# Near-row search end in a written-out order, bias by chunks, near sums from product 20, and a carry row outside the rank pool

## The chip, the cores and the metric

The kernel runs on one core of a Trainium2 chip. The metric is the device time of one execution in microseconds (us). Three timed executions of the kernel before took 1072.16, 1079.40 and 1079.82 us; their median, 1079.4 us, is the time before. A separate execution was profiled; all times of single instructions come from it.

## The reference

Four graph layers in a row on N = 2708 nodes with 128 features, each followed by a residual sum and a layer norm. The adjacency matrix `adj` is dense in memory, and every layer multiplies by it. Layer 0 is the one around this change:

```python
def _lap_mul(A, x):
    d = 1.0 / jnp.sqrt(jnp.sum(A, axis=-1))
    return d[:, None] * (A @ (d[:, None] * x))
z = jax.nn.leaky_relu(_lap_mul(A, x) @ W1 + b1, negative_slope=0.1)
sq = jnp.sum(z * z, axis=-1)
d2 = jnp.maximum(sq[:, None] + sq[None, :] - 2.0 * (z @ z.T), 0.0)
S = jnp.exp(-jnp.sqrt(d2 + 1e-10) / 2.0)
S = jnp.where(ranks_of_minus_S < 4, S, 0.0)      # the 4 nearest rows of each row
out = _lap_mul(S + A, x) @ W2 + b2
x = layernorm(x + out)
```

Layer 1 is an attention layer, `H = A @ (att @ (x W))` with `att = den / (A @ den)` and `den = exp(leaky_relu(r_i + c_j))`. Layer 2 is a normalized product with `A`, a linear map and a bias; layer 3 is `relu([x, A @ x] @ W.T + b)`.

## The kernel before, in words

**Tiling.** Rows lie in T = 22 tiles of 128 (the last, tile 21, has 20 rows). The columns of `adj` are cut into C = 6 chunks of 512, 512, 512, 512, 384 and 276; a chunk holds 4, 4, 4, 4, 3 and 3 tiles. Six row tiles of `adj` stay in SBUF (`res`); the other sixteen stream through a ring of four slots (`ring`), one slot a panel of four row tiles by one chunk.

**Search (lines 672 to 708).** For each row tile TensorE makes a row block of keys (L689, L699), ScalarE copies it out (L700, three `key` buffers), and VectorE takes the eight largest (L701, `near`) and where they lie (L702, `where`). The last row tiles searched are 16, 17, 18, 19 and 20. `weigh(ts)` turns the four best keys of a group of tiles into similarities `sim` (L596 and L597 on VectorE, L598 to L600 on ScalarE), adds them to the degree (L602, L603), takes the inverse root `d2inv` (L604, L605), scales the rows, `y2` (L607 on GpSimd, or L260 on VectorE for the last group), and stores them to the DRAM tensor `y2_rows` (L615, L619: GpSimd's queue, or ScalarE's for the last group). `others(ts)` (L561 to L589) takes the row itself out of the four and writes the three others' indices back to `where`. `weigh` is called for tiles 0 to 16, 17 to 19, and 20 to 21. Here a scheduler places VectorE's instructions in an order of its own.

**Second product of layer 0 (`by_panels`, lines 202 to 229 and 956 to 1013).** For each chunk, 22 products with `y2` are accumulated; a list of due times, `Due`, counts one tick for each product, and work is hung on ticks (`at(n, f)`). The order of TensorE, VectorE and ScalarE is as written here. `sum_near(t)` gathers the three other near rows of each row of tile t from `y2_rows` by indirect DMA on GpSimd (L729) and sums them on VectorE (L738, L742). It is due at tick `24 + 23 t // 5`. When a chunk's products are done, `end_pass2` sets the tick `n` of its `finish`, never before the tick of its last tile's near sum plus 3; `finish` adds the near sums into the chunk's accumulator on TensorE (`add_near`, L749). At later ticks follow the linear map and the norm (`norm0`: L780, L785), the transposes (L798), the column terms (`find_c`, L852, L857) and the comparisons by which layer 1 ranks its columns (L884, L894, L902, L907). `add_bias(b2_sb)` (L774, L265) adds the bias to all rows of `xs` in one VectorE instruction ahead of this loop.

**Rank stage (lines 1077 to 1475).** It sorts rows into blocks and sums carry rows over the lines of `adj` in two halves (`add_line`, L1360). `end_half(h)` copies the sums from PSUM into `heads` (L1380, L1381), a tile of the pool `rank` with both halves side by side, and `send_half` (L1389) moves them by four DMAs into `carry`: half 0 on ScalarE's queue, half 1 on SP's at the end of the stage.

**Block loop (`block_layer`).** 44 steps: TensorE makes `num` (L1627), ScalarE its inverse (L1481, L1484), VectorE three operations on it (L1491, L1495, L1498), TensorE adds up (L1506). Its tiles come from the pool `own`, which takes the space of `rank` once that is closed, so a first write there waits for the last readers of what lay there. Then `two_layers` runs layers 2 and 3 with `by_panels`. The tile `m_rows` has the tag `hT`, one buffer that `hT`, `head`, `first` and `hot_in` use one after the other.

Of the kernel before, what the change touches and what calls it, by code (L numbers as in the profile page):

```python
# [26 lines left out]
DIST_EPS = 1e-10  # L27
# [3 lines left out]
class Due:  # L31
# [5 lines left out]
    def at(self, n, f, *args):  # L37
        self.work.append((n, len(self.work), f, args))
        self.work.sort(key=lambda w: w[:2])
# [13 lines left out]
def kernel(  # L53
# [16 lines left out]
    nc = tc.nc  # L70
    N, D = x.shape
    assert D == P
    T = (N + P - 1) // P
# [13 lines left out]
    HALF = N // 2  # L87
# [13 lines left out]
    chunk_tiles = [range(a // P, (a + w + P - 1) // P) for a, w in zip(starts, cw)]  # L101
# [24 lines left out]
    xs = big.tile([P, T, D], F32, tag="xs", name="xs")  # L126
# [23 lines left out]
    def row_tile(name):  # L150
        return big.tile([P, T * D], F32, tag="hT", name=name)
# [112 lines left out]
    def add_bias(b):  # L264
        nc.vector.tensor_add(xs, xs, b[:, None, :].to_broadcast([P, T, D]))  # L265
# [95 lines left out]
    sim = near_pool.tile([P, T, TOPK], F32, tag="sim", name="sim")  # L361
    y2_rows = dram.tile([N, D], F32, tag="y2_rows", name="y2_rows")
    xw_rows = dram.tile([N, D], F32, tag="xw_rows", name="xw_rows")
    with tc.tile_pool(name="knn", bufs=1) as knn:
        nsq = knn.tile([P, T], F32, tag="nsq", name="nsq")
# [195 lines left out]
        def others(ts, engine):  # L561

            t0, t1 = ts[0], ts[-1] + 1
            n = t1 - t0
            wf, eq, sm = near[:, t0:t1, :TOPK], near[:, t0:t1, TOPK:], sim[:, t0:t1, :]
            own = own_sim[:, t0:t1]
            four = slot_e[:, : 4 * n].rearrange("p (t k) -> p t k", k=4)
            three = slot_e[:, : 3 * n].rearrange("p (t k) -> p t k", k=3)  # L570
            nc.scalar.copy(wf, where[:, t0:t1, :TOPK])
            nc.vector.tensor_tensor(
                eq, wf, node[:, t0:t1, None].to_broadcast([P, n, TOPK]), op=ALU.is_equal
            )
            engine.tensor_mul(four, eq, sm)  # L575
            engine.tensor_add(own, four[:, :, 0], four[:, :, 1])
            for k in (2, 3):
                engine.tensor_add(own, own, four[:, :, k])
            for k in (1, 2, 3):
                engine.tensor_add(eq[:, :, k], eq[:, :, k - 1], eq[:, :, k])  # L580
            for v in (wf, sm):
                engine.tensor_sub(three, v[:, :, 1:], v[:, :, :3])
                engine.tensor_mul(three, three, eq[:, :, :3])
                engine.tensor_add(v[:, :, :3], v[:, :, :3], three)
            engine.tensor_copy(where[:, t0:t1, TOPK : TOPK + 3], wf[:, :, :3])
            for t in ts:
                engine.tensor_scalar(
                    lone[: pw[t], t : t + 1], eq[: pw[t], t - t0, 3:], -1.0, 1.0, op0=ALU.mult, op1=ALU.add
                )  # L589

        def weigh(ts):

            t0, t1 = ts[0], ts[-1] + 1
            nr, sm = near[:, t0:t1, :TOPK], sim[:, t0:t1, :]

            nc.vector.tensor_add(nr, nr, nsq[:, t0:t1, None].to_broadcast([P, t1 - t0, TOPK]))  # L596
            nc.vector.tensor_scalar(nr, nr, 0.0, DIST_EPS, op0=ALU.min, op1=ALU.subtract)  # L597
            nc.scalar.activation(sm, nr, AF.Ln, scale=-1.0)  # L598
            nc.scalar.activation(sm, sm, AF.Exp, scale=0.5)
            nc.scalar.activation(sm, sm, AF.Exp, scale=-0.5)  # L600
            dd = d2inv[:, t0:t1]
            nc.vector.tensor_reduce(dd, sm, AX.X, ALU.add)  # L602
            nc.vector.tensor_add(dd, dd, deg[:, t0:t1])  # L603
            nc.scalar.activation(dd, dd, AF.Ln)  # L604
            nc.scalar.activation(dd, dd, AF.Exp, scale=-0.5)  # L605
            if t1 < T:
                nc.gpsimd.tensor_mul(  # L607
                    y2[:, t0:t1, :], xs[:, t0:t1, :], d2inv[:, t0:t1, None].to_broadcast([P, t1 - t0, D])
                )
            else:  # L610
                scale_rows(y2, xs, d2inv, ts)
                spread(y2[:, FULL, :])
            full = min(t1, FULL)
            queue = nc.gpsimd if t1 < T else nc.scalar
            queue.dma_start(  # L615
                y2_rows[t0 * P : full * P, :].rearrange("(t p) d -> p t d", p=P), y2[:, t0:full, :]
            )
            if full < t1:
                queue.dma_start(y2_rows[FULL * P :, :], y2[:LAST, FULL, :])  # L619
            else:  # L620
                for a in range(t0, t1, 11):
                    others(range(a, min(a + 11, t1)), nc.gpsimd)

        QUARTER = N // 4
        assert N % 4 == 0 and CW < QUARTER <= 2 * CW
# [45 lines left out]

        ready = [load_panel(g, 0) for g in range(G)]
        tc.keep_in_program_order(nc.scalar.preload_act_table_set("natural_log_exp_and_others"))
        with tc.tile_pool(name="keys", bufs=3) as keys:

            for n, t in enumerate([*range(4, S), *range(4), *range(S, FULL)]):
                p = pw[t]
                if n == 1:
                    best = search_few()
                if n == 3:  # L680
                    join_few(best)
                z2 = small.tile([P, P], F32, tag="z", name="z2")
                nc.scalar.mul(z2[:, :p], zT[:, t * P : t * P + p], 2.0)

                key = keys.tile([P, N], F32, tag="key", name="key")
                pks = [acc_tile() for _ in range(C)]
                def norms(c):
                    cs = cols[c]
                    nc.tensor.matmul(pks[c][:p, : cw[c]], lhsT=ones3[:, :p], rhs=nsq3[:, cs], start=True, stop=False)  # L689


                if n:
                    for c in range(C):
                        norms(c)
                for c in range(C) if n else (5, 3, 2, 4, 1, 0):
                    if not n:
                        norms(c)
                    cs = cols[c]
                    nc.tensor.matmul(pks[c][:p, : cw[c]], lhsT=z2[:, :p], rhs=zT[:, cs], start=False, stop=True)  # L699
                    nc.scalar.copy(key[:p, cs], pks[c][:p, : cw[c]])  # L700
                nc.vector.max(near[:p, t, :], key[:p])  # L701
                nc.vector.max_index(where[:p, t, :], near[:p, t, :], key[:p])  # L702
                if t == T - 6:
                    weigh(range(0, T - 5))
                if t == T - 3:
                    weigh(range(T - 5, T - 2))
            weigh(range(T - 2, T))
            others(range(T - 2, T), nc.vector)

    psum.close()  # L710
    acc_pool = psum.enter_context(tc.tile_pool(name="acc1", bufs=3, space=bass.MemoryType.PSUM))
# [59 lines left out]
    spare = near.rearrange("p t k -> p (t k)")  # L771
    few_n, rk_f, neg_r = (spare[:, n * T : (n + 1) * T] for n in range(3))
    nc.vector.memset(rows_d, 0.0)
    add_bias(b2_sb)  # L774
    rk = rk_pool.tile([P, T], F32, tag="rk", name="rk")

    def norm0(ts, raw=False):
# [177 lines left out]

    due = Due()
    at = due.at
    near_at = [24 + (23 * t) // 5 for t in range(T)]
    for t in range(T):
        at(near_at[t], sum_near, t)  # L960
    at(20, nc.vector.memset, rk_f, float(OOB))

    ended = [-16]
# [98 lines left out]
    rows = {}  # L1062
# [14 lines left out]
    with tc.tile_pool(name="rank", bufs=1) as rank:  # L1077
        def rtile(shape, name, dt=F32):
            return rank.tile([P] + shape, dt, tag=name, name=name)
# [295 lines left out]
        def end_half(h):  # L1375

            if not carries:
                carries.append(big.tile([P, NQ * P], F32, tag="y", name="carry"))
            tot = heads[:, h * span : (h + 1) * span]
            nc.scalar.copy(tot[:, : edges[4] - edges[3]], banks[h][:, : edges[4] - edges[3]])  # L1380
            nc.scalar.copy(tot[:64, edges[4] - edges[3] :], banks[h][:64, edges[4] - edges[3] : span])  # L1381
            if h == 0:
                send_half(h, tot, nc.scalar)

        def send_half(h, tot, queue):

            for g in range(4):
                w = edges[g + 1] - edges[g]
                queue.dma_start(  # L1389
                    carries[0][HEADS : HEADS + 2 * NCH, h * HALF + edges[g] : h * HALF + edges[g + 1]],  # L1390
                    tot[32 * g : 32 * g + 2 * NCH, :w],
                )
# [39 lines left out]

        work["groups"] = 0
        nc.vector.tensor_reduce(lone_part, lone, AX.X, ALU.add)
        heads = rtile([2 * span], "heads")
        loaded, held = [0], [0]

        def line(n):
# [24 lines left out]
        ]  # L1463
        for f, *args in turns:
            f(*args)
        end_half(1)
        carry = carries[0]
        assert loaded[0] == 2 * S and held[0] == 2 * (FULL - S) and work["groups"] == 6
        xws, lw = work["xws"], work["lw"]
        load(0)  # L1470
        load(1)
        send_half(1, heads[:, span:], nc.sync)
        for c in range(C):
            nc.sync.dma_start(res[few(c), FULL - S, cols[c]], adjT[FULL * P :, cols[c]])
        order.close()
# [35 lines left out]
    WIDE = 2 * CW  # L1511
    NARROW = HALF - WIDE
    assert 0 < NARROW <= CW

    m_rows = row_tile("m_rows").rearrange("p (t d) -> p t d", d=D)
    mT = m_rows.rearrange("p t d -> p (t d)")[:, :N]

    mixed = carry.rearrange("p (t d) -> p t d", d=D)
    EARLY = HALF // P
# [301 lines left out]
```

## Time and profile before

| | us |
|---|---|
| median of three executions | 1079.4 (1072.16 to 1079.82) |
| profiled execution, its own time | 1053.01 |
| its span, first to last instruction | 1051.3 |
| PE busy | 981.7 (93%) |
| DVE busy | 637.8 (61%) |
| ACT busy | 331.6 (32%) |
| POOL busy | 265.4 (25%) |

PE is TensorE, PEld its weight load, DVE VectorE, ACT ScalarE, POOL GpSimd, SP the engine whose queue issues most DMAs. A busy share is an average over stages. In the profiled execution the search ends at about 294 us, the second product of layer 0 runs from 288 to 424, the rank stage to 493, the block loop to about 715, and the rest is layers 2 and 3. A line of the timeline gives the start in us, the duration, the engine, the line of the kernel, the operation, output and inputs with their sizes, and in brackets the idle time before it with the work that ended the wait.

### The profile page before, as it was taken

The page shows a single profiled execution, that of the slowest core. Times are in us where ns is not written, and L with a number is a line of the kernel's source. Part 1 is how long each engine was busy: PE and PEld are TensorE (multiplying, and loading weights), DVE is VectorE, ACT ScalarE, POOL GpSimd, SP SyncE. Part 2 cuts the span into 40 slices and gives each one's busy share as a digit, 9 for nine tenths or more (in the row PEclk, how much of TensorE's full clock was granted, in tenths as well). Part 3 has the DMA queues.
Part 4 walks back from the last instruction along what each step waited for, and adds up shares of the span by engine and source line. Part 5 has one row for each costly group of instructions (what it writes and reads, how often), then busy time and mean ns, then how long its engine had stood idle before and what let it go on. Part 6 is the DMA issues. An engine that isn't in the chain of part 4 may idle for free.

```text
span 1051.3 us, 11657 instructions
## 1 busy us (share of the span) xinstructions
PE 981.7 (93%) x3773; PEld 481.5 (46%) x3773; DVE 637.8 (61%) x1358; ACT 331.6 (32%) x609; POOL 265.4 (25%) x339
## 2 busy tenths in 40 slices
PE   0898999999997998799899999999999999999996
PEld 0346554444443566554333333334445544564444
DVE  5885438999954668764999999994121121222222
ACT  0000125555501245503777777662010100010000
POOL 4000000000377774007666444420121100000000
PEclk9899999999999999699899999999999999999998
DMA  9997350000086756596565455566665956584652
GB/s 337 355 364 262 113 174 1 0 1 1 1 269 198 227 182 208 201 410 206 144 168 154 138 138 169 137 172 221 201 206 161 316 164 220 146 277 163 220 173 70
DMA packets 102001, 191.00 MB, mean 182 GB/s; under 512 B 14022, under 2 KB 43342, under 8 KB 101930
## 3 DMA queue, kind: packets, MB, share of 16 engines
q1 hardware_dynamic: 83896, 152.34, 43.5%
q0 software_dynamic: 17728, 37.62, 12.9%
q8 instruction: 32, 0.52, 0.2%
q14 instruction: 39, 0.32, 0.1%
q10 hardware_dynamic: 306, 0.20, 0.1%
HBM read 214.80 MB, written 4.16 MB: 208 GB/s over the span
## 4 chain that ended last, share of the span: by engine, by line
PE 72%; DVE 16%; DMA 6%; ACT 2%; issue 2%; POOL 1%; SPq 1%; POOLq 0%; DVEq 0%; ACTq 0%
PE acc L204 34%; PE hacc L1506 10%; PE num L1627 10%; PE acc L428 7%; DVE where L702 6%; DVE near L701 5%; DMA res<-in_adjT 3%; PE acc L1360 3%; DMA got<-y_rows,where 1%; PE mis L285 1%; PE acc L699 1%; DMA part<-in_adjT 1%; DVE both L483 1%; POOL ring L125 1%; PE mis L1090 1%
## 5 line engine op out<-in xcount | busy, mean ns | idle before, releaser
L1068 POOL DMA_INDIRECT ring<-in_adjT,slot_i x88 | 93.7, 1065 | 96.2 <-PE num L1627 77.4
L1627 PE MATMUL num<-ring,lw 128*64 128x512 f32 (+1 forms) x528 | 112.7, 560 | 5.3 <-DVE err L1491 4.7
L1506 PE MATMUL hacc<-inv,xws 128*128 128x512 f32 (+1 forms) x264 | 112.0, 560 | 0.3 <-DVE inv L1498 0.3
L699 PE MATMUL acc<-zT,z 128*128 128x512 f32 (+2 forms) x252 | 102.2, 552 | 0.0
L1481 ACT ACTIVATE inv<-num,plain 128x1024 f32<-128x1024 f32 x88 | 80.6, 916 | 59.8 <-PE num L1627 42.9
L253 POOL TENSOR_TENSOR rstd<-rstd,minus_half 128x4 f32<-128x4 f32 (+1 forms) x18 | 17.3, 961 | 311.8 <-DVE rstd L252 311.8
L234 ACT COPY gb<-acc 128x512 f32<-128x512 f32 (+2 forms) x18 | 9.6, 536 | 249.4 <-PE acc L204 249.4
L700 ACT COPY key<-acc 128x512 f32<-128x512 f32 (+2 forms) x126 | 67.1, 535 | 55.1 <-issue 27.9
L1506 PEld LDWEIGHTS hacc<-inv,xws 128*128 128x128 f32 x264 | 46.7, 190 | 78.1 <-issue 33.7
L204 PE MATMUL acc<-ring,y 128*128 128x512 f32 (+2 forms) x192 | 81.3, 554 | 0.5 <-issue 0.5
L1491 DVE TENSOR_TENSOR err<-inv,num 128x1024 f32<-128x1024 f32 x88 | 74.7, 854 | 11.0 <-ACT inv L1484 9.8
L729 POOL DMA_INDIRECT got<-y_rows,where x66 | 71.7, 1087 | 26.3 <-issue 9.1
L1498 DVE SCALAR_TENSOR_TENSOR inv<-gb,g_inv,inv 128x1024 f32<-128x1024 f32 x88 | 77.0, 913 | 0.1
L204 PE MATMUL acc<-ring,xs 128*128 128x512 f32 (+2 forms) x192 | 76.7, 542 | 0.0
L204 PE MATMUL acc<-ring,carry 128*128 128x512 f32 (+2 forms) x192 | 74.5, 542 | 0.0
L204 PE MATMUL acc<-ring,m_rows 128*128 128x512 f32 (+2 forms) x192 | 74.3, 542 | 0.0
L1495 DVE SCALAR_TENSOR_TENSOR inv<-err,inv 128x1024 f32<-128x1024 f32 x88 | 72.5, 862 | 0.1
L699 PEld LDWEIGHTS acc<-zT,z 128*128 128x128 f32 x252 | 45.8, 190 | 50.4 <-issue 45.0
L1484 ACT ACTIVATE inv<-inv 128x1024 f32<-128x1024 f32 x88 | 67.6, 768 | 2.8
L575 POOL TENSOR_TENSOR slot_e<-near,sim 128x44 f32<-128x44 f32 (+2 forms) x3 | 0.7, 243 | 267.8 <-DVE d2inv L603 265.7
L1627 PEld LDWEIGHTS num<-ring,lw 128*64 128x64 f32 x528 | 36.8, 138 | 62.5 <-issue 44.4
L701 DVE MAX8 near<-key 128x8 f32<-128x2708 f32 x21 | 62.3, 2965 | 2.7 <-ACT key L700 2.7
(376 smaller groups left out, 1369.8 us busy)
## 6 DMA issues: line engine op xcount, KB each, us to landing
ring<-in_adjT SPq DMA_DIRECT2D x74, 1024.0 KB
ring<-in_adjT SPq DMA_DIRECT2D x20, 677.0 KB
ring<-in_adjT SPq DMA_DIRECT2D x17, 768.0 KB
part<-in_adjT SPq DMA_DIRECT2D x12, 1024.0 KB
ring<-in_adjT SPq DMA_DIRECT2D x17, 552.0 KB
more<-in_adjT SPq DMA_DIRECT2D x10, 677.0 KB
res<-in_adjT SPq DMA_DIRECT2D x4, 1280.0 KB
part<-in_adjT SPq DMA_DIRECT2D x3, 768.0 KB
```

Source lines behind the costliest of these rows:

```text
L204: nc.tensor.matmul(accs[c][: lhsT.shape[-1], :w], lhsT=lhsT, rhs=src, start=start, stop=stop)
L428: nc.tensor.matmul(accs[c][:, : cw[c]], lhsT=y[:, i, :], rhs=src[:, : cw[c]], start=first, stop=last)
L699: nc.tensor.matmul(pks[c][:p, : cw[c]], lhsT=z2[:, :p], rhs=zT[:, cs], start=False, stop=True)
L701: nc.vector.max(near[:p, t, :], key[:p])
L729: nc.gpsimd.indirect_dma_start(out=got[:p, :], out_offset=None, in_=y2_rows[:, :], in_offset=bass.IndirectOffsetOnAxis(ap=where[:p, t, k : ...
L1068: nc.gpsimd.indirect_dma_start(out=rows[i][:KC, n, :], out_offset=None, in_=adj_half[:, :], in_offset=bass.IndirectOffsetOnAxis(ap=slot_i[ ...
L1481: nc.scalar.activation(inv, num[:, :w], AF.Ln, scale=plain[:, 0:1], bias=plain[:, 1:2])
L1491: nc.vector.tensor_mul(err, inv, num[:, :w])
L1495: nc.vector.scalar_tensor_tensor(inv, err, 2.0, inv, op0=ALU.subtract, op1=ALU.mult)
L1498: nc.vector.scalar_tensor_tensor(inv, gb[:, col : col + w], g_inv[:, q : q + 1], inv, op0=ALU.max, op1=ALU.mult)
L1506: nc.tensor.matmul(haccs[:, o:e], lhsT=xws[:, q, :], rhs=inv[:, o:e], start=(q == 0), stop=(q == NQ - 1))
L1627: nc.tensor.matmul(num[n * (BJ + 2) : (n + 1) * (BJ + 2), o:e], lhsT=lw[:, 2 * q + n, :], rhs=rows[i][:, n, c0 + o : c0 + e], start=True, ...
```

## The change

Five things are edited.

1. `weigh` is cut into `weigh_near` (L596 to L600; it now writes to `sim` and leaves `near` as it was), `find_d2` and `keep_y2`. From row tile 16 on, VectorE's order is the written one (`manual_schedule` for the vector engine alone). `weigh_near` of a group stands between the L701 and the L702 of the group's last searched tile; for tiles 20 and 21, `find_d2` and `keep_y2` stand there too. `others` of tiles 0 to 16 follows `keep_y2` of its group, and that of tiles 17 to 19 is called after `weigh_near` of the last group.
2. The bias is added by chunks, `add_b2`, six VectorE instructions hung on the tick of the chunk's first near sum.
3. Near sums are due from tick 20 on instead of 24, 4.8 ticks apart instead of 4.6.
4. `heads` becomes a list: half 0 in a tile of half the former size in the pool `rank`, half 1 in a part of `m_rows`.
5. `m_rows` and `mT` are therefore made before `end_half(1)`.

```diff
-        def weigh(ts):
+        def weigh_near(ts):
             t0, t1 = ts[0], ts[-1] + 1
             nr, sm = near[:, t0:t1, :TOPK], sim[:, t0:t1, :]
-            nc.vector.tensor_add(nr, nr, nsq[:, t0:t1, None].to_broadcast([P, t1 - t0, TOPK]))
-            nc.vector.tensor_scalar(nr, nr, 0.0, DIST_EPS, op0=ALU.min, op1=ALU.subtract)
-            nc.scalar.activation(sm, nr, AF.Ln, scale=-1.0)
+            nc.vector.tensor_add(sm, nr, nsq[:, t0:t1, None].to_broadcast([P, t1 - t0, TOPK]))
+            nc.vector.tensor_scalar(sm, sm, 0.0, DIST_EPS, op0=ALU.min, op1=ALU.subtract)
+            nc.scalar.activation(sm, sm, AF.Ln, scale=-1.0)
             nc.scalar.activation(sm, sm, AF.Exp, scale=0.5)
             nc.scalar.activation(sm, sm, AF.Exp, scale=-0.5)
+
+        def find_d2(ts):
+            t0, t1 = ts[0], ts[-1] + 1
             dd = d2inv[:, t0:t1]
-            nc.vector.tensor_reduce(dd, sm, AX.X, ALU.add)
+            nc.vector.tensor_reduce(dd, sim[:, t0:t1, :], AX.X, ALU.add)
...
+        def keep_y2(ts):
+            t0, t1 = ts[0], ts[-1] + 1
             if t1 < T:
...
                 queue.dma_start(y2_rows[FULL * P :, :], y2[:LAST, FULL, :])
-            else:
-                for a in range(t0, t1, 11):
-                    others(range(a, min(a + 11, t1)), nc.gpsimd)
...
+        ends = ExitStack()
...
+                if t == T - 6:
+                    ends.enter_context(tc.manual_schedule(engines={nc.vector.engine}))
                 nc.vector.max(near[:p, t, :], key[:p])
+                if t == T - 6:
+                    weigh_near(range(0, T - 5))
+                if t == T - 3:
+                    weigh_near(range(T - 5, T - 2))
+                if t == T - 2:
+                    weigh_near(range(T - 2, T))
+                    others(range(T - 5, T - 2), nc.gpsimd)
+                    find_d2(range(T - 2, T))
+                    keep_y2(range(T - 2, T))
                 nc.vector.max_index(where[:p, t, :], near[:p, t, :], key[:p])
+                if t == T - 3:
+                    find_d2(range(T - 5, T - 2))
+                    keep_y2(range(T - 5, T - 2))
                 if t == T - 6:
-                    weigh(range(0, T - 5))
-                if t == T - 3:
-                    weigh(range(T - 5, T - 2))
-            weigh(range(T - 2, T))
+                    find_d2(range(0, T - 5))
+                    keep_y2(range(0, T - 5))
+                    for a in range(0, T - 5, 11):
+                        others(range(a, min(a + 11, T - 5)), nc.gpsimd)
             others(range(T - 2, T), nc.vector)
+            ends.close()
...
-    add_bias(b2_sb)
...
-    near_at = [24 + (23 * t) // 5 for t in range(T)]
+    near_at = [20 + (24 * t) // 5 for t in range(T)]
+
+    def add_b2(ts):
+        rows = xs[:, ts[0] : ts[-1] + 1, :]
+        nc.vector.tensor_add(rows, rows, b2_sb[:, None, :].to_broadcast([P, len(ts), D]))
+
     for t in range(T):
         at(near_at[t], sum_near, t)
+    for ts in chunk_tiles:
+        at(near_at[ts[0]], add_b2, ts)
...
-            tot = heads[:, h * span : (h + 1) * span]
+            tot = heads[h]
...
-        heads = rtile([2 * span], "heads")
+        heads = [rtile([span], "heads")]
...
+        m_rows = row_tile("m_rows").rearrange("p (t d) -> p t d", d=D)
+        mT = m_rows.rearrange("p t d -> p (t d)")[:, :N]
+        heads.append(mT[:, HALF : HALF + span])
         end_half(1)
...
-        send_half(1, heads[:, span:], nc.sync)
+        send_half(1, heads[1], nc.sync)
```

More of the change, by code (lines that the diff above doesn't have):

```diff
@@ L1513 @@
     assert 0 < NARROW <= CW
-    m_rows = row_tile("m_rows").rearrange("p (t d) -> p t d", d=D)
-    mT = m_rows.rearrange("p t d -> p (t d)")[:, :N]
     mixed = carry.rearrange("p (t d) -> p t d", d=D)
```

## The prediction

> **What bounds the kernel now.** I read the page's busy times first, then TensorE's waits from 285 to 420 us, the timeline around the longest of them, the granted clock there, and the timeline where the block loop begins.
>
> ```profile
> span 1051.3 us, 11657 instructions
> PE 981.7 (93%) x3773; PEld 481.5 (46%) x3773; DVE 637.8 (61%) x1358; ACT 331.6 (32%) x609; POOL 265.4 (25%) x339
> PE 72%; DVE 16%; DMA 6%; ACT 2%; issue 2%; POOL 1%; SPq 1%; POOLq 0%; DVEq 0%; ACTq 0%
> ```
>
> TensorE is busy for 93% of the span, so an edit elsewhere can win only TensorE's idle time, or time in a stage where another engine leads. Two such places touch the diff. The first is in the second product of layer 0. From the timelines of VectorE, GpSimd and TensorE:
>
> ```profile
> 298.77 3.09 DVE L265 TENSOR_TENSOR xs<-xs,b 128x2816 f32<-128x2816 f32 x1 [1.61 <-POOL y L607]
> 298.84 3.08 POOL L585 CAST where<-near 128x9 uint32<-128x9 f32 x1
> 301.86 0.85 POOL L615 DMA_DIRECT2D y_rows<-y  x1
> 306.41 1.15 POOL L729 DMA_INDIRECT got<-y_rows,where  x1 [3.17 <-DMA y_rows<-y]
> 323.39 0.49 PE L749 MATMUL acc<-ident,near_sum 128*128 128x128 f32 x2 [1.93 <-DVE near_sum L742]
> 327.44 0.79 PE L749 MATMUL acc<-ident,near_sum 128*128 128x128 f32 x2 [3.56 <-DVE near_sum L742]
> ```
>
> A nine-element cast, 0.20 us elsewhere, lasts as long as the bias add beside it; behind it stands the store of tiles 17 to 19, and no gather may begin before all rows are stored. TensorE then waits 1.93 and 3.56 us for the near sums of tiles 2 and 3. The stretches after that, busy time by engine, with the granted clock as the third figure from the end:
>
> ```profile
> 327.40:329.00 1.60, 1.56 (x4) 1.05 (x5) 0.94 (x4) 0.71 (x2) 1.02 (x2) 0.50 0.20 54
> 329.00:331.00 2.00, 2.00 (x6) 0.88 (x5) 0.32 (x1) 1.15 (x1) 1.69 (x2) 0.68 0.26 70
> ```
>
> The clock is 0.50 of full speed, then 0.68. The second place is the start of the block loop, from the timelines of TensorE, ScalarE, SP and VectorE:
>
> ```profile
> 493.10 3.29 SPq L1389 DMA_DIRECT2D carry<-heads  x4
> 493.17 4.31 PE L1627 MATMUL num<-ring,lw 128*64 128x512 f32 x20 [0.66 <-ACT heads L1381]
> 493.23 1.28 ACT L1617 ACT_TABLE_LOAD   x1 [0.15 <-issue]
> 498.08 1.20 ACT L1481 ACTIVATE inv<-num,plain 128x1024 f32<-128x1024 f32 x1 [3.57 <-DMA res<-in_adjT]
> 500.46 1.63 DVE L1491 TENSOR_TENSOR err<-inv,num 128x1024 f32<-128x1024 f32 x2 [8.38 <-ACT inv L1484]
> ```
>
> ScalarE holds the table and the first sums, and waits 3.57 us for a DMA. By the waits built into the program these are the four sends of half 1, because `inv` lies where `heads` lay. From 500.46 on VectorE leads (148.5 of 150 us busy from 550 to 700), so each us there counts in full.
>
> **What the Trainium skill says.** "SBUF — State Buffer", section "Who interferes with whom": a VectorE instruction with two SBUF inputs and a GpSimd one that reads SBUF exclude each other for a whole instruction. The trace agrees: 3.08 beside 3.09 us. "TensorE: Matmul & The Clock Gate", section "What's actually happening": an idle window of about 3.4 us halves the clock. The trace shows 0.50 after a wait of 3.56 us. "DMA: Bandwidth & Descriptors", section "Anatomy of one DMA — SWDGE (gpsimd) path": some 2 us are fixed, most of it until the write is confirmed. Here 2.86 us pass from the end of the store's issue (302.71) to its landing (305.57 by the chain of waits), and 1.66 from the last send's issue (496.39) to 498.05.
>
> **Part 1, search end.** The search itself cannot get shorter: TensorE runs one row tile in 5.99 us without a gap (L689 and L699) and ends at 287.24 in both kernels. VectorE's order changes. The L701 of tile 16 ends at 267.05; L596 and L597 (0.21 + 0.18) follow, then L702 to 270.4. Now stands a new wait: the second L572 needs ScalarE's L571 for tiles 11 to 16, which needs that L702 and is queued behind the first key copy of tile 18 (271.67 + 0.59). It ends near 272.5, and behind the waiting L572 stands the L701 of tile 17: 272.6 instead of 270.05, a lag of 2.6. Three pairs at 5.96 and the pieces for tiles 17 to 19 (0.7) bring the L701 of tile 20 to 291.2, its end to 294.1. Who waits for that lag? A key buffer is free when the L702 three tiles earlier ends: tile 17's ends at 278.6, tile 20's first copy was at 283.6, so the lag is covered by 5.0 us; beyond that TensorE would stall one for one.
>
> For tiles 20 and 21 the weights no longer wait for the last L702. From L597 to L260 took 1.96 us (294.75 to 296.71); now L597 stands at 294.25, L260 ends at 296.65 instead of 297.16. ScalarE's two stores follow at once (0.36 + 0.60): end of issue 297.7. Tiles 17 to 19 get `d2inv` at 291.7 and are stored by GpSimd at about 293, ahead of the `others` of their group and free of the bias add. GpSimd's own queue, `others` of 17 to 19, starts at 294.7 and takes 3.4 us without that cast: free at 298.1. So the last landing is now ScalarE's store. The trace has no landing of that queue's store; I bound it by 1.66 and 2.86 and take 2.86, as it writes DRAM among panel loads: 300.5. Then 0.84 us, as before (305.57 to 306.41): the first gather at 301.4, 5.0 earlier. The last L702, now ending near 299.7, and eighteen small operations after it are done by 302, before the first rows arrive (306).
>
> Gathers come one per 1.31 us whatever precedes them, so near sum 3 ends at 327.4 - 5.0 = 322.4.
>
> **Part 2, near sums from product 20.** Tile 3 becomes due at 34, so chunk 0's `finish` at 37 instead of 40: three products of 0.86 us less stand before it, and TensorE asks at 320.86 - 2.58 = 318.28. Three tiles take 1.1 us, then it waits from 319.4 to 322.4: 3.0 instead of 5.49. It resumes products at 323.0; before it was at 328.02 with three products more, worth 325.44. Gain 2.45. The slow clock cost 1.6 x 0.50 + 2.0 x 0.32 = 1.4; a wait of 3.0 is just under the window, so I count half: 0.7. Together 3.15.
>
> **Part 3, bias by chunks.** One add of 3.09 for 2816 elements becomes 0.56 four times and 0.42 twice, the same sum. The first four stand where VectorE idled before L785 (2.64, 4.50, 2.54 us) or L742. That of chunk 4 falls into a busy run that ended with 1.15 idle. That of chunk 5 falls into the run from 399.38, which is on the chain: 0.42 lost. Against it chunk 3's `finish` comes one product (0.65) earlier, 95 for 96. Net gain 0.2. Gathers have a lead by then, so a collision of 0.56 with GpSimd costs nothing.
>
> **Part 4, carry row.** ScalarE's first L1481 now needs the table (494.51) and eight of the twenty matmul records (493.17 + 8 x 0.2155 = 494.9): 3.1 earlier than 498.08. Half 0 still lies in the pool, but its sends were issued by 478.1. SP's queue is unmoved, and so is the next item it owes: carry rows for step 2, issued 498.86 to 500.27, landing near 501.9. From there `num` takes 1.3 to 2.6, the inverse 2.27: 505.5 to 506.8. VectorE asks at 497.35 + 9.52 = 506.9. In time. Step 2 also had a wait of 0.75 (511.94), with TensorE's clock at 0.50 after 4.67 idle; half of it may go, 0.4. Together 3.5. The copy into `m_rows` waits for `hot_in`, read last near 481: nothing.
>
> **Sum.** 3.15 + 0.2 + 3.5 = 6.9 us. The profiled execution took 1053.0 (span 1051.3 and 1.7 around it): 1046.1 after. The median of the timed runs is 2.5% above that execution; I take the 6.9 off it: 1072.5.
>
> **Rivals.** *More (0.25).* The store lands in 1.66: gathers at 300.2, a wait of 1.8, gain 3.65 + 1.4 clock + 0.2 + 3.85 = 9.1: 1070.3. For: the store is 74 KB. Against: DMA engines are full until about 303. *Less (0.18).* Gathers at 303.8 and step 2 short of its rows by 1.5: 0.2 + 1.6 = 1.8: 1077.6. For: the bounds above touch. *Slower (0.07).* One mechanism: ScalarE's store lies behind the panels (DMA share 0.97 to 1.00 at 316 to 323). Because `finish` asks 2.58 earlier, gathers after 303.9 already lose in part 2, and after 307.6 in the sum, one us per us; at 312 it is 1083.8. Against: GpSimd's store landed in 2.86. That half 1's wait stays is excluded by the built waits.
>
> **Numbers.** Likeliest 0.50. A measurement tells about 1% (10.8 us) from no change; the three runs before spread over 0.7%. Faster by over 1% needs 1068.6: half of *more*, a quarter of the likeliest by spread, a little of *less*: 0.28. Slower: 0.05. The range, 1063 to 1082, takes in the first three cases with the spread and leaves out *slower*.
>
> **What would show it.** Right: the first L729 at about 301; one wait of about 3 us at chunk 0's near sums, clock 1.00 after; the first inverse at 1.7 us after the first `num`. Wrong: VectorE's L701 of tile 17 held past 275, the first gather after 304, or a new wait at step 2.

## The result and the profile after

Eight timed executions of the kernel after have a median of 1067.31 us (1059.94 to 1072.01), eight of the kernel before one of 1078.77 (1072.16 to 1080.47). The ratio is 0.9906, 95% interval [0.9879, 0.9933]: 11.5 us by the medians, against 6.9 forecast, and by the ratio within the 1% that counts as no change. The predicted 1072.5 was 5.2 us too high.

The profiled execution of the kernel after took 1068.27 us. That of the kernel before, 1053.01, lay 2.4% below its timed ones and is not one of them, so the two spans can't be subtracted; the stages have to be compared. The page:

```profile
span 1066.5 us, 11660 instructions
PE 983.9 (92%) x3773; PEld 481.8 (45%) x3773; DVE 637.6 (60%) x1363; ACT 331.9 (31%) x609; POOL 264.9 (25%) x339
PE 48%; DVE 1%; ACT 1%; issue 0%; DMA 0%; POOL 0%; SPq 0%; POOLq 0%
```

TensorE does the same work in a span 15 us longer. (The chain of waits, the page's last line, covers only half of this span; I don't build on it.) The timelines of VectorE, GpSimd, TensorE and ScalarE from the end of the search to chunk 0's norm, where all times are 0.99 later than before, counted from the first product (288.75 for 287.76):

```profile
273.34 0.18 DVE L572 TENSOR_TENSOR near<-near,node 128x24 f32<-128x24 f32 x1 [1.41 <-ACT near L571]
273.44 2.97 DVE L709 MAX8 near<-key 128x8 f32<-128x2708 f32 x1
293.66 0.86 POOL L623 DMA_DIRECT2D y_rows<-y  x1 [0.31 <-POOL y L615]
298.17 0.19 POOL L585 CAST where<-near 128x9 uint32<-128x9 f32 x1
302.20 1.18 POOL L750 DMA_INDIRECT got<-y_rows,where  x1 [3.40 <-DMA y_rows<-y]
319.27 0.83 PE L770 MATMUL acc<-ident,near_sum 128*128 128x128 f32 x6
322.77 0.49 PE L770 MATMUL acc<-ident,near_sum 128*128 128x128 f32 x2 [2.67 <-issue]
336.10 0.58 ACT L1000 COPY hT<-acc 128x512 f32<-128x512 f32 x1 [35.60 <-remote]
336.74 2.08 PE L800 MATMUL mis<-w,hT 128*128 128x128 f32 x8 [11.76 <-ACT hT L1000]
```

The cast takes 0.19 us instead of 3.08, the store of tiles 17 to 19 goes out 8.2 us earlier, the first gather 4.2 us earlier (5.2 counted from the first product), and one wait of 2.67 us stands where 1.93 and 3.56 were. Then something that nothing in the change accounts for: ScalarE copies `hT` 12.8 us after TensorE is done with that chunk (its last line on it ends at 323.26), and TensorE, which goes on with the next chunk for a while, waits 11.76 us. The trace has no work that released ScalarE then.

The start of the block loop, timelines of SP, TensorE, ScalarE and VectorE:

```profile
507.43 3.18 SPq L1416 DMA_DIRECT2D carry<-m_rows  x4
510.65 1.26 SPq L1504 DMA_DIRECT2D res<-in_adjT  x3
513.08 1.42 SPq L1102 DMA_DIRECT2D ring<-carry  x2
507.50 4.31 PE L1654 MATMUL num<-ring,lw 128*64 128x512 f32 x20 [0.66 <-issue]
509.62 1.20 ACT L1511 ACTIVATE inv<-num,plain 128x1024 f32<-128x1024 f32 x1 [0.78 <-PE num L1654]
512.00 1.63 DVE L1521 TENSOR_TENSOR err<-inv,num 128x1024 f32<-128x1024 f32 x2 [4.90 <-DMA carry<-m_rows]
```

The first inverse starts 2.12 us after the first `num` instead of 4.91, without the wait for the sends. The carry rows of step 2 (L1102) are issued 5.58 us after it, where they were 5.69 before. In this execution step 2 is in time all the same, in TensorE's timeline:

```profile
513.68 0.78 PE L1654 MATMUL num<-ring,lw 128*64 128x330 f32 x4 [1.88 <-DVE err L1521]
515.26 2.66 PE L1654 MATMUL num<-ring,lw 128*64 128x512 f32 x8 [0.81 <-DMA ring<-carry]
```

VectorE starts step 2's first `err` without a wait, 14.02 us after the first `num` (16.81 before).

### The profile page after: what moved, and what is told of

Same layout as the page of the kernel before. It is cut to its first block, busy times and chain, and to the rows that moved or that the text cites. A ratio compares the mean times of both kernels' runs of the same rounds, so it can differ in the third digit from the quotient of the medians.

```text
span 1066.5 us, 11660 instructions
## 1 busy us (share of the span) xinstructions
PE 983.9 (92%) x3773; PEld 481.8 (45%) x3773; DVE 637.6 (60%) x1363; ACT 331.9 (31%) x609; POOL 264.9 (25%) x339
## 3 DMA queue, kind: packets, MB, share of 16 engines
q0 software_dynamic: 17728, 37.62, 12.8%
## 4 chain that ended last, share of the span: by engine, by line
PE 48%; DVE 1%; ACT 1%; issue 0%; DMA 0%; POOL 0%; SPq 0%; POOLq 0%
PE acc L204 27%; PE hacc L1536 10%; PE num L1654 9%; PE mis L285 1%; PE mis L1783 0%; DMA ring<-carry 0%; ACT gb L234 0%; PE mis L1749 0%; DVE inv L1525 0%; PE mis L1779 0%; DVE inv L1528 0%; ACT inv L1511 0%; POOL rstd L253 0%; DVE err L1521 0%; PE mis L1737 0%
## 5 line engine op out<-in xcount | busy, mean ns | idle before, releaser
L1095 POOL DMA_INDIRECT ring<-in_adjT,slot_i x88 | 96.6, 1098 | 93.8 <-PE num L1654 72.1
L709 DVE MAX8 near<-key 128x8 f32<-128x2708 f32 x21 | 62.3, 2965 | 2.6 <-ACT key L706 2.6
```

What stands on the lines that cost most here:

```text
L1095: nc.gpsimd.indirect_dma_start(out=rows[i][:KC, n, :], out_offset=None, in_=adj_half[:, :], in_offset=bass.IndirectOffsetOnAxis(ap=slot_i[ ...
```

## The experiments

The runs were made on four chips. There the kernel before took 1054.2 to 1055.5 us in the median, not 1078.8; on which chip the result above was measured is not known. Differences in microseconds are the ratio's distance from 1 times 1055, brackets are 95% intervals, and a ratio is always to the kernel before on the same chip.

**Both kernels once more.** No edit. The profiles are to tell which waits belong to the change.

> The kernel before, unchanged, for a second profile. Its first profiled execution took 1053.0 us, 2.4% under the median of its timed runs (1078.8). Theory A (that execution was an exception): the span is 1070 to 1078 now, and one or two stalls of 5 to 15 us stand on TensorE which the first profile did not have and which no recorded work explains. Theory B (a profiled execution is as a rule that much faster): the span is 1050 to 1055 again with the same waits, 1.93 and 3.56 us at the near sums of chunk 0, and 4.67 us at step 2 of the block loop.

> The kernel after, unchanged, for a second profile. In its first one ScalarE copied hT of chunk 0 at 336.10, 11.6 us after TensorE had finished that chunk, and TensorE waited 11.8 us. Theory A (the stall is an accident of that execution): it is gone, the span is about 12 us shorter or lies elsewhere, and the rest is as before: one wait of about 3 us at chunk 0's near sums. Theory B (the change makes the stall): ScalarE is 11 to 12 us late at the same copy again.

Measured: 1057.6 and 1055.4 us. The 11.8 us wait is gone from the kernel after, and no profile of any later run has it: theory A, the change by itself doesn't make the stall. It may not have been an accident of one execution, for all eight of that measurement took 1059.94 us or more, and the same kernel has a median of 1051.43 below. For the kernel before it is the number of theory B (span 1055.8, 0.8 us above its range, with one wait of 4.93 us at chunk 0), but not its reason: the timed executions on this chip take 1054.2 us too, so a profiled one isn't faster as a rule, and the 1079 us belong to where or when they were measured.

**The kernel after, timed again.** No edit.

> The kernel after, unchanged, timed again. By the second pair of profiles the change moves chunk 0's end 1 to 3 us and the block loop between -0.4 and 3 us. Theory A (that is all of it; the 11.5 us first measured came from stalls that fell differently in the two kernels, on the chip of that day): ratio 0.995 to 0.999. Theory B (the whole 11.5 us belong to the change): ratio 0.9906 again, within 0.988 to 0.993.

Measured: median 1051.43 against 1055.22, ratio 0.9969 [0.9949, 0.9988], so 3.3 us (1.3 to 5.4). Theory A, as to the size. The 6.9 us forecast lie outside this interval.

**Part 1 alone.** Parts 2 to 4 are undone in the kernel after:

```diff
-    near_at = [20 + (24 * t) // 5 for t in range(T)]
+    near_at = [24 + (23 * t) // 5 for t in range(T)]
...
-    for ts in chunk_tiles:
-        at(near_at[ts[0]], add_b2, ts)
...
+    add_bias(b2_sb)          # ahead of the loop
...
-        heads = [rtile([span], "heads")]
+        heads = rtile([2 * span], "heads")
...
```

> The kernel before with only the end of the search in the written order (part 1; near sums due from tick 24, bias in one piece, both halves of the carry row in the rank pool). By the prediction's own numbers part 1 takes the first gather 5.0 us forward and the wait at chunk 0 from 5.5 us to about 0.5: 5.0 us faster, ratio 0.9953. Since the profiles showed the first gather 13.4 to 15.4 us after the first product of the pass instead of 18.4, I expect 3 to 5: ratio 0.995 to 0.997. Rival (part 2 was needed for it, the gain is not there alone): 0.999 or more.

Measured: 1049.75 against 1055.25, 0.9949 [0.993, 0.9968]: 5.4 us faster. By the middle values part 1 alone is worth more than the whole change was in its second timing (the two intervals overlap). TensorE's wait at chunk 0, from its timeline:

```profile
323.11 0.49 PE L770 MATMUL acc<-ident,near_sum 128*128 128x128 f32 x2 [0.42 <-DVE near_sum L763]
```

0.42 us are left of 5.49, and the clock stays at 1.00 behind it.

**Part 2 undone, and part 2 alone.** In the kernel after:

```diff
-    near_at = [20 + (24 * t) // 5 for t in range(T)]
+    near_at = [24 + (23 * t) // 5 for t in range(T)]
```

> The kernel after with the near sums due from tick 24, 4.6 ticks apart, as before (part 2 undone). By the prediction chunk 0's finish is then asked for three products (2.58 us) later, so the wait for near sums of chunk 0 falls from 3 to 4.5 us to 0.4 to 2 us, and the end of chunk 0 is at the same moment: within 1 us of the kernel after. Rival: the earlier asking is what wins (the products of chunk 1 fill the wait less well): 2 to 2.6 us slower.

Measured: 1049.23 against 1055.22, 0.9937 [0.9919, 0.9955]: 3.4 us *faster* than the kernel after on the same chip (six executions; the intervals just overlap). Neither expectation held. The first overlooked that at the same end of chunk 0 three more products are done. So the reverse edit, in the kernel before:

```diff
-    near_at = [24 + (23 * t) // 5 for t in range(T)]
+    near_at = [20 + (24 * t) // 5 for t in range(T)]
```

> The kernel before with only the near sums due from tick 20, 4.8 ticks apart (part 2). The gathers still begin 18.4 us after the first product. Theory (from the kernel with part 2 undone, which was faster): chunk 0's finish is asked for 2.58 us earlier but cannot end earlier, so the wait there grows from 5.5 to about 8 us, the clock after it is halved as before, and the kernel is 2 to 3 us slower, ratio 1.002 to 1.003. Rival (part 2 brings the gathers or the later chunks forward by itself): ratio 0.999 or less.

Measured: 1058.27 against 1055.51, 1.0025 [1.0013, 1.0037]: 2.6 us slower. TensorE's timeline:

```profile
320.44 0.61 PE L749 MATMUL acc<-ident,near_sum 128*128 128x128 f32 x4
323.18 0.49 PE L749 MATMUL acc<-ident,near_sum 128*128 128x128 f32 x2 [2.13 <-DVE near_sum L742]
327.68 0.79 PE L749 MATMUL acc<-ident,near_sum 128*128 128x128 f32 x2 [4.01 <-DVE near_sum L742]
```

The waits add up to 6.14 us, not the 8 expected: in this execution the gathers took 4.1 us from issue to landing (median), in the two profiles of the kernel before 5.8 and 5.2. TensorE asks 2.58 us earlier (30.52 us after the pass's first product for 33.10), can't finish the chunk before the gathers, and has three products less behind it. By the time measured, part 2 costs what the prediction's working has for it, 2.55 us.

**Part 3 undone.**

```diff
+    add_bias(b2_sb)          # ahead of the loop
...
-    for ts in chunk_tiles:
-        at(near_at[ts[0]], add_b2, ts)
```

> The kernel after with the bias added in one VectorE instruction ahead of the loop, as before (part 3 undone). The add (3.1 us, two SBUF inputs) then stands behind the others of tiles 20 and 21, at about 303 to 306, when GpSimd gathers. Theory: it delays near sum 0 by at most 1 us and no gather, so the time is that of the kernel after within 1 us. Rival: it holds GpSimd's descriptor writing for 3 us and the last gathers of chunk 0 with it: 2 to 3 us slower.

Measured: 1052.66, 0.9979 [0.9962, 0.9997], against 0.9969 for the kernel after. The intervals overlap for most of their length: part 3 is worth 1 us or nothing, and the rival's 2 to 3 us are not there. In the profile the first gather starts 13.44 us after the first product, as in the best runs with the bias by chunks.

**Part 4 alone, and part 4 undone.** In the kernel before, and the reverse in the kernel after:

```diff
-            tot = heads[:, h * span : (h + 1) * span]
+            tot = heads[h]
...
-        heads = rtile([2 * span], "heads")
+        heads = [rtile([span], "heads")]
...
+        heads.append(mT[:, HALF : HALF + span])
         end_half(1)
```

> The kernel before with only the carry row of half 1 moved out of the rank pool (parts 4 and 5 of the change). The prediction's step: the first inverse of the block loop starts 1.7 us after the first num product instead of 4.9, and the time falls by 3.1 to 3.5 us (ratio 0.997). Rival: step 2 is short of its carry rows, issued behind the four sends on SP's queue; the gain is 1.6 us or less and a wait of 1 to 3 us for that DMA stands at num(2). Rival: the measured gain of the whole change, about 10 us, is mainly here: ratio 0.993 or less.

> The kernel after with the carry row of half 1 back in the rank pool (parts 4 and 5 undone). By the prediction part 4 is worth 3.5 us: this kernel is 3.5 us slower than the kernel after (ratio to the kernel before 0.997). By the rival, which the run of part 4 alone supports (ratio 1.0015), part 4 is worth nothing: the same time as the kernel after within 1.5 us, the first inverse 4.9 us after the first num, and no wait of VectorE for carry rows at step 2 beyond the 0.75 us of the kernel before.

Measured: alone 1055.70 against 1054.19, 1.0015 [1.0002, 1.0028], so 1.6 us slower and not 3.3 faster. Undone: 1054.73, 1.0005 [0.998, 1.0029], which taken against 0.9969 would make part 4 worth 3.8 us. The two contradict each other, and no total here settles it. Those fourteen executions scatter from 1049.6 to 1065.3, and in the profiled one the loss is ahead of the block loop: the first `num` 205.90 us after the first product of the second pass, against 201.33 in the timed kernel after, with a wait of 4.41 us at chunk 0. The stage itself is clearer than the totals. This is what all profiles but those of the last three runs show (us; the gather and chunk 1's near sums from the pass's first product, the inverse and the `err` operations from the first `num`; "third" and "fifth" are the wide `err` of steps 2 and 4):

| | first gather | waits at chunk 0 | chunk 1 | first inverse | third | fifth |
|---|---|---|---|---|---|---|
| before | 18.65 | 1.93, 3.56 | 60.55 | 4.91 | 16.81 | 27.32 |
| before again | 18.16 | 4.93 | 60.84 | 4.88 | 16.78 | 27.17 |
| part 4 alone | 18.29 | 5.64 | 60.54 | 2.12 | 15.21 | 25.81 |
| part 2 alone | 18.09 | 2.13, 4.01 | 59.70 | 4.70 | 16.60 | 26.28 |
| part 1 alone | 13.55 | 0.42 | 53.84 | 4.70 | 16.60 | 27.34 |
| after | 13.45 | 2.67 | disturbed | 2.12 | 14.02 | 25.10 |
| after again | 14.98 | 4.47 | 57.00 | 2.12 | 16.30 | 27.58 |
| after, timed | 13.57 | 1.71 | 53.03 | 2.15 | 16.52 | 27.65 |
| part 2 undone | 15.44 | 2.33 | 55.94 | 2.11 | 16.45 | 27.36 |
| part 3 undone | 13.44 | 2.20 | 54.63 | 2.15 | 16.11 | 27.45 |
| part 4 undone | 15.17 | 4.41 | 57.45 | 5.75 | 17.65 | 27.91 |

Part 4 takes the first inverse some 2.8 us forward every time (2.11 to 2.15, where it is 4.70 to 5.75 without). By the fifth `err` the mean of the six with it is 26.8, of the five without it 27.2: 0.4 us are left, in values that range from 25.10 to 27.91. Where the rest goes is seen in the timed kernel after, timelines of SP, TensorE and VectorE:

```profile
488.96 3.18 SPq L1416 DMA_DIRECT2D carry<-m_rows  x4
492.18 1.27 SPq L1504 DMA_DIRECT2D res<-in_adjT  x3
494.62 1.42 SPq L1102 DMA_DIRECT2D ring<-carry  x2
489.03 4.34 PE L1654 MATMUL num<-ring,lw 128*64 128x512 f32 x20 [0.66 <-ACT m_rows L1408]
495.25 0.78 PE L1654 MATMUL num<-ring,lw 128*64 128x330 f32 x4 [1.87 <-DVE err L1521]
496.81 1.39 PE L1654 MATMUL num<-ring,lw 128*64 128x512 f32 x2 [0.79 <-DMA ring<-carry]
499.54 3.65 PE L1654 MATMUL num<-ring,lw 128*64 128x512 f32 x6 [1.34 <-DMA ring<-carry]
505.55 1.22 DVE L1521 TENSOR_TENSOR err<-inv,num 128x1024 f32<-128x1024 f32 x1 [2.39 <-ACT inv L1514]
508.13 0.50 DVE L1521 TENSOR_TENSOR err<-inv,num 128x330 f32<-128x330 f32 x1 [1.36 <-ACT inv L1514]
```

And in its chain of waits there, and in the stretches of time (columns as the header line says):

```profile
495.45 3.95 DMA ring<-carry
```

```profile
core 0: us, PE busy (x) PEld busy (x) DVE busy (x) ACT busy (x) POOL busy (x), PEclk, DMA share, GB/s
498.20:499.50 1.30, 0.00 (x0) 0.00 (x0) 1.30 (x3) 0.00 (x0) 1.00 (x2) 0.50 0.37 128
500.50:503.20 2.70, 2.70 (x7) 0.47 (x3) 2.66 (x4) 0.00 (x0) 1.47 (x1) 0.50 0.82 263
```

SP has four sends and three loads of the last row tile to issue, then reads the value of `flag` (L1547) and branches on it, and is at it without a gap from 488.96 to 494.6. (Of the six loads that the program names here, three stand over 100 us earlier in SP's queue.) Only then come step 2's carry rows, and the second pair of them lands at 499.40. TensorE has waited 1.87, 0.79 and 1.34 us by then, its clock is at 0.50, and it takes 3.65 us over the last six records. VectorE waits 2.39 + 1.36 = 3.75 us at step 2: more than the 2.76 that the inverse had won.

The queue explains the late issue, but not all of the lateness, for in the recorded execution of the kernel after the rows were issued just as late and step 2 didn't wait. GpSimd's timeline, there and in the timed kernel after, has the first gather for step 3 (step 2's own gathers are issued before the loop begins):

```profile
513.19 1.10 POOL L1095 DMA_INDIRECT ring<-in_adjT,slot_i  x1 [0.21 <-issue]
493.43 1.10 POOL L1095 DMA_INDIRECT ring<-in_adjT,slot_i  x1 [0.21 <-PE num L1654]
```

That is 5.69 us after the first `num` in the recorded execution and 4.40 in the other. In the traces' DMA packets, the second pair of carry rows moves from 7.64 to 8.07 us after the first `num` in the first case, and from 9.13 to 9.53 in the second, after many packets of those gathers, which begin at 6.19 there (at 7.48 in the first case). The ten profiles with the gather at 4.4 and the rows issued near 5.6 all have that pair between 8.88 and 9.63, that of the kernel before too. So the rows seem to come late by two things, the queue ahead of their issue and the gathers beside their transfer. For the second there is one execution against ten and no run that changes it alone, so it is not shown.

**SP's queue cleared.** From the kernel with part 2 undone, the four sends and the six loads (seven of these ten stood ahead of the rows in the traces) are taken out of the way:

```diff
-        send_half(1, heads[1], nc.sync)
-        for c in range(C):
-            nc.sync.dma_start(res[few(c), FULL - S, cols[c]], adjT[FULL * P :, cols[c]])
...
                     if i + 2 < len(steps):
                         load(i + 2)
+                    if 4 <= i < 8:
+                        send_half(1, heads[1], nc.sync, [i - 4])
+                    if 8 <= i < 8 + C:
+                        few_rows(i - 8)   # the load above, one chunk
```

> The kernel after with near sums due from tick 24, and SP's queue at the start of the block loop cleared: the four sends of half 1 go out one at a step in steps 4 to 7, the six loads of the last row tile in steps 8 to 13, so the carry rows of step 2 no longer stand behind ten DMAs (5.6 us). Theory A (those rows made step 2 late, and so ate part 4's gain): VectorE's third err starts 14.0 to 15 us after the first num instead of 16.4, TensorE's clock stays near 1.00 there, and the kernel is 1.5 to 2.5 us faster than the one with near sums due from tick 24 (ratio to before 0.9915 to 0.993). Theory B (the gathers of GpSimd, issued behind its 3.9 us power operation, end last anyway): third err at 15.5 or later, less than 1 us gained.

Measured: 1047.36 against 1055.25, 0.9902 [0.9866, 0.9938]. With part 2 undone alone it was 0.9937 [0.9919, 0.9955]; the intervals overlap, and by the medians the two kernels lie 7.9 and 6.0 us below the kernel before, so the stage is the better witness. Its timelines of SP, TensorE and VectorE:

```profile
486.66 2.44 SPq L1102 DMA_DIRECT2D ring<-carry  x2
493.17 4.31 PE L1656 MATMUL num<-ring,lw 128*64 128x512 f32 x20 [0.66 <-ACT m_rows L1408]
499.36 2.50 PE L1656 MATMUL num<-ring,lw 128*64 128x330 f32 x12 [1.88 <-DVE err L1518]
507.19 1.62 DVE L1518 TENSOR_TENSOR err<-inv,num 128x1024 f32<-128x1024 f32 x2
```

Theory A. The rows are issued before the loop begins, TensorE runs in 2.50 us at full clock the twelve records that took from 495.25 to 503.19 in the timed kernel after, the third `err` starts 14.02 us after the first `num` without a wait, and the fifth at 24.15: 3.2 us earlier than 27.36. At the last of the 44 steps the 3.2 us are still there (215.08 for 218.27). That is about what part 4 was forecast to bring (3.5), once the rows go out early. The gathers of step 3 start 1.0 us earlier here too (3.36 after the first `num`); with the rows already landed they delay nothing.

**GpSimd's power operation moved too**, and then near sums from tick 27:

```diff
+                    if i == 20:
+                        inv_sqrt_of(dinv, deg, DEG_EPS)
...
-        inv_sqrt_of(dinv, deg, DEG_EPS)   # in two_layers
```

> The same with GpSimd's power operation (3.9 us, for layer 2's row scales) moved from ahead of the loop to step 20, so that the gathers of step 2 too go out at once. Theory A (SP's queue alone mattered): the same as without this edit within 0.7 us. Theory B (gathers end last): third err at 14.0, no wait of TensorE for rows, and 1 to 2.5 us faster than without this edit.

Measured: 1046.03, again 0.9902 [0.9864, 0.9939]. The fifth `err` starts at 23.63, 0.5 us earlier, and TensorE waits for no rows, but at the last step nothing of it is left (215.20 for 215.08). Theory A: with the rows out early, the gathers hardly matter. (The gathers behind the power operation are those of step 3; step 2's are issued before the first `num` in both kernels, 5.5 and 3.2 us in the first and 4.4 and 2.2 us in the second.)

```diff
-    near_at = [24 + (23 * t) // 5 for t in range(T)]
+    near_at = [27 + (22 * t) // 5 for t in range(T)]
```

> The same with near sums due from tick 27, 4.4 ticks apart: chunk 0's finish is asked for three products later than with tick 24. Theory (as long as TensorE waits there for gathers, every product put ahead of that wait is won whole): the wait at chunk 0 shrinks by up to 2.6 us to nothing, and the kernel gains 0.5 to 2.3 us. Rival (later near sums push chunks 4 and 5, whose column terms VectorE bounds): no gain, or up to 1 us slower.

Measured: 1048.28, 0.9912 [0.988, 0.9944]. No gain: in the profile with tick 24 the wait at chunk 0 was gone already, and there was nothing left to win. The kernel with the power operation moved and tick 24 has the lowest median of the study, though it isn't told apart from the one with SP's queue cleared alone. It beats both kernels (0.9902 [0.9864, 0.9939] and 0.9969 [0.9949, 0.9988] don't overlap), 9 us below the kernel before by the medians (1046.03 against 1055.25); the kernel after, on another chip, was 3.8 below (1051.43 against 1055.22).

## Why the prediction came out as it did

The number held, with luck; the search's end came as worked out. The sum was a mixture of one good step, one loss booked inside it, and one gain that is mostly not there. A range of 19 us let 1067.31 in, but the forecast gain of 6.9 us lies in neither interval: 7.2 to 13.1 us in the first measurement, 1.3 to 5.4 in the second.

- **Search end (L709 of tile 17, the stores, the first gather).** Right step by step. Less the 0.99 us, tile 17's L709 starts at 272.45 (forecast 272.6), and the first gather at 301.2 (301.4). The lag, 2.4 us as it came, cost TensorE nothing: the pass begins as in the kernel before. The one term on the edge was the landing of ScalarE's store. I took 2.86 us as its upper bound, which with 0.84 makes 3.70 to the gather; the ten profiles with part 1 have 3.84 to 5.47 from the end of its issue. The Trainium skill, "DMA: Bandwidth & Descriptors", section "Latency and other measured facts", has access to HBM go from 0.2 us on average to 2 us under high load; the spread of 1.6 us here fits, though no run varied the load alone. Part of it is seen: in the four latest profiles ScalarE's issue of its second store took 0.97 to 1.02 us, in the six others 0.59 to 0.60, and the packets of the two stores moved over 2.2 to 2.6 us instead of 0.7 to 1.2. Why the issue is slow at times stays open. The gathers come 3 to 5 us earlier rather than always 5. ScalarE's timeline, kernel after, first and second profile:

```profile
297.76 0.60 ACTq L627 DMA_DIRECT2D y_rows<-y  x1
298.54 0.99 ACTq L627 DMA_DIRECT2D y_rows<-y  x1
```

- **The rival *less*, with its gathers at 303.8.** Four of the ten profiles went most of the way there (14.98 to 15.44 us after the first product; 301.4 is 13.6 and 303.8 is 16.0), and its other half, step 2 short of its rows, is what five of the six profiles with part 4 show. At 0.18 it was the rival nearest to what the later chips measured.
- **Near sums from 20.** The gain of 2.45 was 5.0 of part 1 less 2.55 that part 2 takes away. The working had it ("three products more, worth 325.44"), but it was booked as one step, and part 2 looked like a help. By itself it costs 2.6 us (1.4 to 3.9), and undoing it won 3.4.
- **The clock.** Half of 1.4 was a fair guess, but for another reason than that the wait is just too short. After waits at chunk 0 of 0.42, 1.71 and 2.33 us the granted clock from 325 to 331 is 1.00; behind each of two waits of 2.20 it is 0.50 for 3.41 us, and behind 4.41 and 4.47 for 6.83 and 3.41. The Trainium skill, "TensorE: Matmul & The Clock Gate", section "What's actually happening", has the activity judged in a window of some 3.4 us that runs freely. The traces agree: within one trace all changes of the clock lie on a grid of 3.41 us. One wait of 2.20 us lies in a single window, the wait of 2.33 us in two (first two lines: the kernel with SP's queue cleared; last two: that with part 2 undone; columns as above):

```profile
322.50:325.91 3.41, 1.21 (x8) 0.78 (x8) 1.06 (x4) 0.25 (x1) 2.50 (x4) 1.00 1.00 345
325.91:329.32 3.41, 3.41 (x9) 1.86 (x8) 1.20 (x3) 1.62 (x2) 2.53 (x3) 0.50 0.53 189
320.84:324.26 3.42, 1.80 (x9) 1.02 (x7) 1.13 (x4) 0.00 (x0) 2.50 (x4) 1.00 1.01 335
324.26:327.67 3.41, 2.70 (x12) 1.74 (x13) 1.25 (x4) 1.87 (x2) 2.64 (x3) 1.00 0.91 326
```

  Where the page speaks of an idle window, a window with TensorE busy for 1.21 us of 3.41 was enough here.
- **Bias by chunks.** 0.2 forecast; 1 us or nothing measured. Not told apart.
- **Carry row.** The first half is right: 2.12 us after the first `num` for 1.7. The step that failed is "landing near 501.9 ... In time". It held in the recorded execution of the kernel after, whose third `err` starts at 14.02; in the five other profiles with part 4 and SP's queue as it was, it starts at 15.21 to 16.52, after a wait. SP's queue was named as unmoved, and the seven DMAs ahead of the rows are in the trace of before; that they would now set the end of step 2 was not. Two terms were too small: from the last issue to the landing 3.4 us (496.04 to 499.40) instead of 1.6, and `num` of step 2, 3.65 us for six records at half clock instead of 1.3 to 2.6 in all. The first could have been read from the trace of before: there the packets of the second pair move until 502.60, so it can't have landed by 501.9. 0.4 us of 3.5 remain in the mean. The undisturbed half, 2.8 us, was taken by a new wait, the very one named as what would show the step wrong. Two readings of the working are loose: 494.9 is 3.2 us before 498.08, not 3.1, and from 550 to 700 us, where VectorE is busy for 148.48 us, TensorE shows as busy for all 150.00, so that VectorE leads there was argued, not shown.
- **The size.** With the parts as measured alone (-5.4, +2.6, about -1 or 0, and -0.4 by the stage or +1.6 by the time), the whole should win 1 to 4 us, and 3.3 were measured in the second timing. In the first it was 11.5. What the first chip adds, some 24 us to the kernel before and some 16 to the kernel after, is open: the one profile from there has 11.76 us in ScalarE's late copy, and of the kernel before no profile of such an execution exists. The profile of before took 1053.01 us, near what the four chips' timings of that kernel give. That the kernel after escapes part of the loss for a reason that lies in the change was neither shown nor excluded, so of the 11.5 us some 8 have no cause shown.

## What to carry to other kernels

When a wait's end is set by a transfer, asking for its result earlier is a loss (2.6 us here): as long as the wait lasts, each product put ahead of it is won whole, so move the transfer forward and the request back. A wait that is removed at the head of a loop uncovers the next item of every queue that feeds step 2; count what stands ahead of that item in the queue, not only whether the queue has moved, and look in the trace of before for when its packets really moved. Book two edits that meet in one wait as two terms, even if one number comes out.

## What the runs showed of the hardware

TensorE's clock can stay low while it is busy. In the profile of part 2 alone, rank stage (columns as above):

```profile
456.00:476.00 20.00, 20.00 (x108) 11.11 (x109) 7.96 (x19) 0.16 (x1) 0.29 (x1) 0.50 1.01 402
```

For 20 us TensorE shows as busy throughout and the granted clock is 0.50. The products show it too: twelve of L1201 take 2.79 us there and 1.53 in the kernel before. In the other profiles the same stretch of work had 3.4 us at half clock; here the first `num` came 7 us later after chunk 5 (78.3 us for 70.6 to 72.4), and that one execution took 1064.6 us where its kernel's median is 1058.3.

Waits are counted together, by windows. In the timed kernel after, the waits of 1.87 and 0.79 us before step 2 left TensorE busy for 1.34 us of the window from 493.97 to 497.38, and the next one is at 0.50; the wait of 1.34 us came only after that. In the two stages of this change, the end of chunk 0 and the first steps of the block loop, the fourteen traces agree on where that turns: after each window at full clock with TensorE busy for 1.44 us or less it was 0.50, after each with 1.49 us or more it stayed at 1.00. That isn't a rule for all work: in the kernel before, where products are small, the window from 422.4 to 425.8 has 2.96 us busy and is followed by 0.50.

Landings scatter more than I had allowed: 4.1 to 5.8 us in the median for the same gathers, 3.84 to 5.47 from the same store's issue to the first gather, so that two profiles of the kernel after differ by 4 us at chunk 1's near sums (53.03 and 57.00).
